# First stage of a three-stage decoder layer: squares and queries split in their PSUM banks, one LayerNorm sequence per tile, its output on ScalarE

## The chip, the cores and the metric

The kernel runs on one core of one Trainium2 chip, as a single launch. The metric is the device time of that launch in microseconds (us). The core has five engines that work side by side, each through its own instructions in a fixed order: TensorE (PE in the profile: matmuls, and PEld for the weight loads that run ahead of them), VectorE (DVE), ScalarE (ACT), GpSimd (POOL) and SyncE (SP), which here only issues DMAs. They hand work to each other by semaphores. SBUF is the working memory; PSUM, of 8 banks, takes the results of the matmuls.

## The reference, cut to what matters

The layer adds three blocks to a residual stream `x` of 4096 tokens by 512 channels. The change touches the first block alone:

```
h   = layernorm(x)                          # no gain, no bias
y   = (h - mean(h)) * rsqrt(var(h) + EPS)   # a second LayerNorm, on h
q   = (y * ln_g + ln_b) split in 4 heads of 128
s   = q @ k.T            # k: w_fc read as 2048 rows of 128
p   = square(relu(s))
x1  = x + (h + p @ v)    # v: w_proj.T read as 2048 rows of 128
```

The second block is attention to a context of 128 tokens, the third a shared and a routed feed-forward block with 32 experts. All is held to float32: a matmul of two float32 numbers is made as three matmuls of rounded parts, high by low, low by high and high by high.

## The kernel before, in words

**Tiles.** The first stage (`stage0`) takes the tokens in 8 tiles `t` of 512. For each tile and each of the 4 heads it runs 16 steps `kt`, one for each 128 rows of `k` and `v`: 512 steps in all. A step makes three matmuls into a PSUM bank `s` (L337), then ScalarE takes the relu into `rl` (L341), VectorE multiplies `s` by `rl` into `p`, which is the square (L343), and `split` parts `p` into a rounded high part `ph` and the rest `pl = p - ph`. Seven steps later (`LAG`) `av` feeds `ph` and `pl` to three matmuls (L298) that add up in the bank `o` of the head. A step is therefore six matmuls of 128 by 512.

**Who splits.** `split` (L93 to L96) makes the high part with a copy on ScalarE (L93), or on VectorE where it is told so (L95), and the low part with a subtraction on VectorE or GpSimd (L96). Of 8 steps in a row the numbers 1, 3, 5, 6 and 7 have the low part on GpSimd; 0, 2 and 4 have it on VectorE, and number 2 has its high part on VectorE too. [...]

**Buffers.** The banks of `s` go by turns: even `kt` have tag `P1`, odd `kt` have `P2`, two banks each; a bank is free for its next block of scores when nothing reads it any more. `p` lies in SBUF under tag `H` with 3 buffers, `rl` under `K` with 2, `ph` and `pl` under `A` and `B` with 8. Two more banks (`P4`) serve all transposes and the context products, two (`P3`) the sums `o`.

**LayerNorms of the next tile.** `prep` makes `y` for the next tile in the middle of the steps of the present one. It is a generator, and the loop over the steps takes one piece of it at a time. The tile has four row blocks of 128 tokens; two generators handle two blocks each, one after the other. A generator loads `x` (L236), takes mean and variance on VectorE (L241, L242), makes both LayerNorms' factors from them in a row of small operations (L246 to L251, the power on GpSimd, L248), writes `y` with VectorE (L254), then has GpSimd form the residual (L264), which SP stores to `x1` (L265). `prep_head` transposes `y` for one head (L272), applies gain and bias on ScalarE from PSUM to an SBUF tile `q` (L274), and splits `q` into `qh` and `ql`. Heads 0 to 2 of the next tile are made in step 12 of heads 1 to 3, the last one in step 8 of the tile itself.

**Background.** In some steps a further generator (`context_steps`) does a piece of preparation for the second stage: it splits weights with ScalarE and GpSimd, and makes products of the context (`ck`, `cv`) on TensorE.

**What sets the order.** A planner orders the instructions of each engine before the run: it goes by the order in which the program states them, by dependences, by free buffers and by its own estimates of durations. `g.after` keeps an instruction behind given ones on the same engine. On the chip each engine then follows its list, and an instruction that waits holds up everything behind it on its engine.

Of the kernel before, what the change touches and what calls it, by code (L numbers as in the profile page):

```python
# [8 lines left out]
F32 = mybir.dt.float32  # L9
# [5 lines left out]
A = mybir.AluOpType  # L15
AF = mybir.ActivationFunctionType
# [9 lines left out]
EPS = 1e-5  # L26
# [14 lines left out]
def f32(ap):  # L41
    return ap.bitcast(F32)
# [37 lines left out]
@contextmanager  # L80
def later(g, n):

    g.tc.cur_priority += n
    yield
    g.tc.cur_priority -= n


def split(g, hi, lo, src, lo_engine=None, hi_engine=None):

    if isinstance(lo_engine, cycle):  # L90
        lo_engine = next(lo_engine)
    if hi_engine is None:
        g.nc.scalar.copy(hi, src)  # L93
    else:
        hi_engine.tensor_copy(hi, src)  # L95
    (lo_engine or g.nc.vector).tensor_tensor(lo, src, f32(hi), A.subtract)  # L96
# [16 lines left out]
def weight_steps(g, dram, nk, width, name, lo_engine=None):  # L113
    hi, lo = ([[g.piece(name + z)[:] for _ in range(width // 512)] for _ in range(nk)] for z in "hl")
    yield from split_steps(g, dram, hi, lo, lo_engine)
    return hi, lo


def part(w, k, c):

    return w[k][c // 4][:, c % 4 * 128:c % 4 * 128 + 128]


def run(steps):

    try:
        while True:
            next(steps)
    except StopIteration as end:
        return end.value  # L130
# [31 lines left out]
def three(terms):  # L162

    (wh, wl), (xh, xl) = terms
    return (wl, xh), (wh, xl), (wh, xh)
# [53 lines left out]
def stage0(g, x, wfcT, wpT, lnT, x1, background):  # L219
    nc = g.nc  # L220
    NT = T // 512
    LAG = 7
    gb = g.c.tile([128, 2, 4], F32, name="gb")
    with later(g, 20):
        nc.sync.dma_start(gb[:], lnT)
    ys, qs = {}, {}

    def prep(t, tiles):

        rows = [slice(t * 512 + s * 128, t * 512 + s * 128 + 128) for s in tiles]
        n = len(rows)
        xt = [g.tile("G", "xt") for _ in rows]
        for v, r in zip(xt, rows):
            nc.sync.dma_start(v[:], x[r, :])  # L236
        yield
        mv = g.sm.tile([128, n, 2], F32, name="am", tag="am")
        for i, v in enumerate(xt):
            s6 = g.small("as", 6)  # L240
            nc.vector.bn_stats(s6[:], v[:])  # L241
            nc.vector.bn_aggr(mv[:, i, :], s6[:])  # L242
            yield
        ve, r0, tt, rs = (g.small("a" + z, 8) for z in "vptr")
        m = 2 * n
        nc.vector.tensor_scalar(ve[:, 0:n], mv[:, :, 1], EPS, None, A.add)  # L246
        nc.vector.tensor_scalar(ve[:, n:m], mv[:, :, 1], 1.0 + EPS, EPS * EPS, A.mult, A.add)
        power = nc.gpsimd.tensor_tensor(r0[:, 0:m], ve[:, 0:m], g.mhalf[:, 0:m], A.pow)  # L248
        nc.vector.scalar_tensor_tensor(tt[:, 0:m], r0[:, 0:m], -0.5, ve[:, 0:m], A.mult, A.mult)
        nc.vector.tensor_tensor(tt[:, 0:m], tt[:, 0:m], r0[:, 0:m], A.mult)  # L250
        nc.vector.scalar_tensor_tensor(rs[:, 0:m], tt[:, 0:m], 1.5, r0[:, 0:m], A.add, A.mult)  # L251
        for i, v in enumerate(xt):
            y = g.tile("C", "y")
            g.mark = nc.vector.tensor_scalar(y[:], v[:], mv[:, i, 0:1], rs[:, n + i:n + i + 1], A.subtract, A.mult)  # L254
            ys[t] = ys.get(t, []) + [y]
            if i % 2:
                yield

        sc, of = g.small("bv", 4), g.small("bp", 4)
        nc.vector.tensor_scalar(sc[:, 0:n], rs[:, 0:n], 1.0, None, A.add)  # L260
        nc.vector.scalar_tensor_tensor(of[:, 0:n], mv[:, :, 0], -1.0, rs[:, 0:n], A.mult, A.mult)
        for i, v in enumerate(xt):
            with g.after(power):
                g.kept = nc.gpsimd.tensor_scalar(v[:], v[:], sc[:, i:i + 1], of[:, i:i + 1], A.mult, A.add)  # L264
            nc.sync.dma_start(x1[rows[i], :], v[:])  # L265
            if i % 2:
                yield

    def prep_head(t, h):
        pt = g.bank("P4", "pt")  # L270
        for s in range(4):
            nc.tensor.transpose(pt[:, s * 128:(s + 1) * 128], ys[t][s][:, h * 128:(h + 1) * 128], g.ident)  # L272
        q = g.tile("J", "q")
        g.q = nc.scalar.activation(q[:], pt[:], AF.Identity, bias=gb[:, 1, h:h + 1], scale=gb[:, 0, h:h + 1])  # L274
        qh, ql = g.tile("E", "qh", FR), g.tile("F", "ql", FR)
        split(g, qh[:], ql[:], q[:])
        qs[t, h] = (qh, ql)

    run(prep(0, range(4)))
    steps = weight_steps(g, wfcT, 4, 512, "kw", cycle((nc.vector, nc.gpsimd)))  # L280
    kw = run(steps)
    prep_head(0, 0)
    prep_head(0, 1)
    with g.after(g.q):
        vw = run(weight_steps(g, wpT, 4, 512, "vw"))
    prep_head(0, 2)
    prep_head(0, 3)

    P, oT, cur = {}, {}, {}

    def av(t, h, kt):
        p = P.pop((t, h, kt))
        if kt == 0:
            cur["o"] = g.bank("P3", "o")
        o = cur["o"]
        j, rb = divmod(kt, 4)
        for n, (w, y) in enumerate(three(([part(v, rb, j) for v in vw], p))):
            nc.tensor.matmul(o[:], w, y[:], start=kt == 0 and n == 0, stop=kt == 15 and n == 2)  # L298
        if kt < 15:
            return  # L300
        oT[h] = g.tile("D", "oT")
        nc.scalar.copy(oT[h][:], o[:])
        if h < 3:
            return
        for s in range(4):
            rows = x1[t * 512 + s * 128:t * 512 + s * 128 + 128, :]
            b = g.tile("IJ"[s % 2] if t < NT - 1 else "G", "b")
            nc.sync.dma_start(b[:], rows)
            pt = g.bank("P4", "pt")
            for hh in range(4):  # L310
                nc.tensor.transpose(pt[:, hh * 128:(hh + 1) * 128], oT[hh][:, s * 128:(s + 1) * 128], g.ident)
            nc.vector.tensor_tensor(b[:], pt[:], b[:], A.add)
            nc.sync.dma_start(rows, b[:])

    steps = [(t, h, kt) for t in range(NT) for h in range(4) for kt in range(16)]
    todo = []
    marks = []
    for i, (t, h, kt) in enumerate(steps):
        if h == 0 and kt == 2 and t + 1 < NT:
            todo = [prep(t + 1, tiles) for tiles in ((0, 1), (2, 3))]  # L320
            for p in todo:
                next(p)
        if todo and (h > 0 or kt > 6):
            with g.after(*marks):
                if next(todo[0], True):
                    todo.pop(0)
        if t > 0 and h > 0 and kt % 8 == 6:
            with g.after(*marks):
                next(background, None)
        if h > 0 and t + 1 < NT and kt == 12:  # L330
            prep_head(t + 1, h - 1)
        if h == 0 and t > 0 and kt == 8:
            prep_head(t, 3)
        s = g.bank(("P1", "P2")[kt % 2], "s")
        j, rb = divmod(kt, 4)
        for n, (w, y) in enumerate(three(([part(k, j, rb) for k in kw], qs[t, h]))):
            nc.tensor.matmul(s[:], w, y[:], start=n == 0, stop=n == 2)  # L337
        if i >= LAG:
            av(*steps[i - LAG])
        r = g.tile("K", "rl")  # L340
        m0 = nc.scalar.activation(r[:], s[:], AF.Relu)  # L341
        p = g.tile("H", "p")
        m1 = nc.vector.tensor_tensor(p[:], s[:], r[:], A.mult)  # L343
        marks = [m0, m1]
        if (t, h, kt) == (NT - 1, 2, 0):
            g.marks = marks
        ph, pl = g.tile("A", "ph", FR), g.tile("B", "pl", FR)
        split(g, ph[:], pl[:], p[:], nc.gpsimd if i % 8 in (1, 3, 5, 6, 7) else None, nc.vector if i % 8 == 2 else None)
        P[t, h, kt] = (ph, pl)
    run(background)  # L350
    for st in steps[len(steps) - LAG:]:
        av(*st)
# [880 lines left out]
```

## Time and profile before

| what | us |
|---|---|
| median of three runs | 2747.65 (2745.44 to 2748.27) |
| the profiled execution | 2744.97, its span in the trace 2743.2 |
| first scores matmul / last of the stage's `o` matmuls start | 17.9 / 813 |
| PE busy over the span | 2681.9 |
| DVE, ACT, POOL busy over the span | 2054.2, 1786.0, 1033.7 |

The span runs from the first to the last instruction. In a group of the profile, the line number comes first, then the engine, the operation, the tile written and the tiles read, the shape, the count, the busy time in us and the mean duration in ns of one, and then the idle time of the engine just before such instructions and what ended it. A line L93, L95 or L96 is that of the helper `split`, so the tile names tell which split is meant. A matmul's recorded duration (0.39 us for one of 512 columns) is longer than the distance at which the next one starts (0.227 us), since they are pipelined: a busy PE includes that overlap.

### The profile page before, as it was taken

The numbers are of one execution on the slowest core, as the hardware profiler recorded it, in microseconds if no ns is written. First come the engines' busy times: TensorE is split into PE (matmuls) and PEld (weight loads), VectorE is DVE, ScalarE is ACT, GpSimd is POOL, SyncE is SP. The second block draws the span as 40 slices with busy tenths as digits, with TensorE's granted clock in tenths as the row PEclk, the third lists the DMA queues.
The fourth block names the chain that finished last, engine by engine and source line by source line (L and its number), as shares of the span: only waits on it lengthen the run. The fifth ranks groups of instructions, "written<-read, shape, count | busy, mean of one in ns | idle before, by whom it ended". The sixth has DMA issues, their size and how long they took to land. (4 is left out here: it accounts for less than half of the span.)

```text
span 2743.2 us, 47449 instructions
## 1 busy us (share of the span) xinstructions
PE 2681.9 (98%) x14788; PEld 2293.6 (84%) x14788; DVE 2054.2 (75%) x4671; ACT 1786.0 (65%) x3995; POOL 1033.7 (38%) x821
## 2 busy tenths in 40 slices
PE   7999999999999999999999999999999999999998
PEld 5877877777878999899997888888889888898886
DVE  8888788888887888888876722243777787778985
ACT  6777777787867777777775111133666676768885
POOL 5686566667653333333330030001223122223331
PEclk9999999999999999999999999999999999999999
DMA  4021112112120222322246222254888999899994
GB/s 141 32 70 70 70 62 72 64 58 81 36 70 33 75 90 90 114 78 91 74 138 207 96 93 101 72 173 109 271 265 277 284 302 298 280 279 287 325 316 140
DMA packets 237999, 396.69 MB, mean 145 GB/s; under 512 B 29376, under 2 KB 67280, under 8 KB 237744
## 3 DMA queue, kind: packets, MB, share of 16 engines
q1 hardware_dynamic: 223024, 366.45, 39.5%
q0 software_dynamic: 14720, 27.19, 5.0%
q8 instruction: 117, 1.92, 0.3%
q14 instruction: 138, 1.13, 0.1%
HBM read 311.67 MB, written 83.83 MB: 144 GB/s over the span
## 5 line engine op out<-in xcount | busy, mean ns | idle before, releaser
L96 DVE TENSOR_TENSOR rl<-raw,rh 128x512 fp32r<-128x512 f32 x768 | 510.5, 711 | 106.2 <-ACT rh L93 98.0
L93 ACT CAST rh<-raw 128x512 fp32r<-128x512 f32 x768 | 440.3, 622 | 135.7 <-DMA raw<-in_rg 82.8
L96 POOL TENSOR_TENSOR pl<-p,ph 128x512 fp32r<-128x512 f32 x320 | 427.4, 1344 | 242.9 <-ACT ph L93 219.0
L343 DVE TENSOR_TENSOR p<-s,rl 128x512 f32<-128x512 f32 x512 | 343.4, 683 | 81.5 <-ACT rl L341 62.0
L93 ACT CAST ph<-p 128x512 fp32r<-128x512 f32 x448 | 277.7, 622 | 153.9 <-DVE p L343 148.3
L341 ACT ACTIVATE rl<-s 128x512 f32<-128x512 f32 x512 | 301.3, 599 | 34.7 <-PE s L337 21.1
L1019 POOL DMA_INDIRECT out_dram<-v,idx x46 | 108.0, 2347 | 424.8 <-ACT v L1017 332.8
L448 ACT ACTIVATE e<-e,nm 128x128 f32<-128x128 f32 x512 | 199.2, 391 | 63.2 <-DVE nm L445 62.8
L451 POOL TENSOR_TENSOR e<-e,ri 128x512 f32<-128x512 f32 x128 | 133.5, 1043 | 245.2 <-DVE ri L449 128.3
L298 PE MATMUL o<-pl,vwh 128*128 128x512 f32 x512 | 208.0, 406 | 11.0 <-DVE pl L96 7.6
L337 PE MATMUL s<-qh,kwl 128*128 128x512 f32 x512 | 207.2, 406 | 7.3 <-DVE p L343 7.0
L337 PE MATMUL s<-qh,kwh 128*128 128x512 f32 x512 | 201.1, 393 | 0.0
L337 PE MATMUL s<-ql,kwh 128*128 128x512 f32 x512 | 201.1, 393 | 0.0
L298 PE MATMUL o<-ph,vwh 128*128 128x512 f32 x512 | 200.7, 392 | 0.0
L298 PE MATMUL o<-ph,vwl 128*128 128x512 f32 x512 | 198.8, 392 | 0.0
L96 DVE TENSOR_TENSOR pl<-p,ph 128x512 fp32r<-128x512 f32 x192 | 185.2, 965 | 16.1 <-ACT ph L93 13.7
L905 POOL DMA_INDIRECT x<-xs,idx x46 | 57.3, 1247 | 312.0 <-DMA raw<-in_rd 171.8
L93 ACT CAST hh<-s 128x512 fp32r<-128x512 f32 x92 | 57.0, 620 | 164.3 <-DVE s L760 117.2
L422 PE MATMUL q<-yh,wql 128*128 128x256 f32 x512 | 149.5, 292 | 2.8 <-DVE v L481 2.6
L422 PE MATMUL q<-yh,wqh 128*128 128x256 f32 x512 | 145.6, 284 | 0.0
L422 PE MATMUL q<-yl,wqh 128*128 128x256 f32 x512 | 145.0, 283 | 0.0
L755 PE MATMUL g<-z,sw 128*128 128x512 f32 x576 | 139.5, 390 | 1.7 <-ACT s L759 1.7
(296 smaller groups left out, 7607.9 us busy)
## 6 DMA issues: line engine op xcount, KB each, us to landing
raw<-in_rg SPq DMA_DIRECT2D x256, 256.0 KB, 5.3
raw<-in_ru SPq DMA_DIRECT2D x256, 256.0 KB, 5.1
raw<-in_rd SPq DMA_DIRECT2D x256, 256.0 KB, 4.7
z<-zT SPq DMA_DIRECT2D x128, 256.0 KB, 5.4
b<-x SPq DMA_DIRECT2D x64, 256.0 KB, 2.6
xt<-in_x SPq DMA_DIRECT2D x32, 256.0 KB, 2.7
x<-xt SPq DMA_DIRECT2D x32, 256.0 KB, 2.0
x<-b SPq DMA_DIRECT2D x32, 256.0 KB, 2.3
```

Of the source, the lines that this page charges most:

```text
L93: g.nc.scalar.copy(hi, src)
L96: (lo_engine or g.nc.vector).tensor_tensor(lo, src, f32(hi), A.subtract)
L298: nc.tensor.matmul(o[:], w, y[:], start=kt == 0 and n == 0, stop=kt == 15 and n == 2)
L337: nc.tensor.matmul(s[:], w, y[:], start=n == 0, stop=n == 2)
L341: m0 = nc.scalar.activation(r[:], s[:], AF.Relu)
L343: m1 = nc.vector.tensor_tensor(p[:], s[:], r[:], A.mult)
L422: nc.tensor.matmul(o[:, i, :], part(w, k, p), y[k // 2][:, k % 2, :], start=n == 0, stop=n == 11)
L448: nc.scalar.activation(e[:, hs], e[:, hs], AF.Exp, bias=nm[:, h:h + 1], scale=0.125, accum_out=su[:, h:h + 1])
L451: nc.gpsimd.tensor_tensor(e4, e4, ri[:].unsqueeze(2).to_broadcast([128, 4, 128]), A.mult)
L755: nc.tensor.matmul(p[:], part(w, k, c), y[k][:], start=n == 0, stop=n == 11)
L905: nc.gpsimd.indirect_dma_start(out=x[rows], out_offset=None, in_=xs, in_offset=bass.IndirectOffsetOnAxis(ap=idx[rows, b + j:b + j + 1], ax ...
L1019: nc.gpsimd.indirect_dma_start(out=out, out_offset=bass.IndirectOffsetOnAxis(ap=idx[rows, b + j:b + j + 1], axis=0), in_=v[rows], in_offse ...
```

## The change

In the steps where VectorE makes the low part (0, 2 and 4 of 8) the square is no longer written to an SBUF tile `p`: it goes back into its own PSUM bank `s`, and both parts are split from there. The other five steps keep `p`. In `prep_head` the query with gain and bias is likewise written back into the bank `pt` and split from there; the tile `q` is gone, so buffers `J` are left to `b`. `prep` treats all four row blocks of a tile as one sequence: one set of small operations on four blocks where there were two sets on two blocks, with the offset `-mean * factor` made for both LayerNorms at once (L251 after). `y` is made by ScalarE as `Identity(x * scale + bias)`; only in the first tile do blocks 1 and 3 stay on VectorE. The loop takes a piece of `prep` in every odd step where it took one in every step.

```diff
-    def prep(t, tiles):
-        rows = [slice(t * 512 + s * 128, t * 512 + s * 128 + 128) for s in tiles]
+    def prep(t):
+        rows = [slice(t * 512 + s * 128, t * 512 + s * 128 + 128) for s in range(4)]
...
-        ve, r0, tt, rs = (g.small("a" + z, 8) for z in "vptr")
-        nc.vector.tensor_scalar(ve[:, 0:n], mv[:, :, 1], EPS, None, A.add)
-        power = nc.gpsimd.tensor_tensor(r0[:, 0:m], ve[:, 0:m], g.mhalf[:, 0:m], A.pow)
...
+        ve, r0, tt, rs, of = (g.small("a" + z, 8) for z in "vptro")
+        nc.vector.tensor_scalar(ve[:, 0:4], mv[:, :, 1], EPS, None, A.add)
+        power = nc.gpsimd.tensor_tensor(r0[:], ve[:], g.mhalf[:], A.pow)
...
+        mean = mv[:, :, 0].unsqueeze(1).to_broadcast([128, 2, 4])
+        nc.vector.scalar_tensor_tensor(of[:].rearrange("p (a n) -> p a n", a=2), mean, -1.0,
+                                       rs[:].rearrange("p (a n) -> p a n", a=2), A.mult, A.mult)
+        if t > 0:
+            yield
         for i, v in enumerate(xt):
             y = g.tile("C", "y")
-            g.mark = nc.vector.tensor_scalar(y[:], v[:], mv[:, i, 0:1], rs[:, n + i:n + i + 1], A.subtract, A.mult)
+            if t == 0 and i % 2:
+                nc.vector.tensor_scalar(y[:], v[:], mv[:, i, 0:1], rs[:, 4 + i:5 + i], A.subtract, A.mult)
+            else:
+                nc.scalar.activation(y[:], v[:], AF.Identity, bias=of[:, 4 + i:5 + i], scale=rs[:, 4 + i:5 + i])
...
-        sc, of = g.small("bv", 4), g.small("bp", 4)
-        nc.vector.scalar_tensor_tensor(of[:, 0:n], mv[:, :, 0], -1.0, rs[:, 0:n], A.mult, A.mult)
+        sc = g.small("bv", 4)
...
-        q = g.tile("J", "q")
-        g.q = nc.scalar.activation(q[:], pt[:], AF.Identity, bias=gb[:, 1, h:h + 1], scale=gb[:, 0, h:h + 1])
+        g.q = nc.scalar.activation(pt[:], pt[:], AF.Identity, bias=gb[:, 1, h:h + 1], scale=gb[:, 0, h:h + 1])
-        split(g, qh[:], ql[:], q[:])
+        split(g, qh[:], ql[:], pt[:])
...
-            todo = [prep(t + 1, tiles) for tiles in ((0, 1), (2, 3))]
+            todo = prep(t + 1)
-        if todo and (h > 0 or kt > 6):
+        if t + 1 < NT and (h > 0 or kt > 6) and kt % 2:
...
-        p = g.tile("H", "p")
+        apart = i % 8 in (1, 3, 5, 6, 7)
+        p = g.tile("H", "p") if apart else s
         m1 = nc.vector.tensor_tensor(p[:], s[:], r[:], A.mult)
...
-        split(g, ph[:], pl[:], p[:], nc.gpsimd if i % 8 in (1, 3, 5, 6, 7) else None, nc.vector if i % 8 == 2 else None)
+        split(g, ph[:], pl[:], p[:], nc.gpsimd if apart else None, nc.vector if i % 8 == 2 else None)
```

More of the change, by code (lines that the diff above doesn't have):

```diff
@@ L226, in stage0 @@
     ys, qs = {}, {}
-    def prep(t, tiles):
-        rows = [slice(t * 512 + s * 128, t * 512 + s * 128 + 128) for s in tiles]
-        n = len(rows)
+    def prep(t):
+        rows = [slice(t * 512 + s * 128, t * 512 + s * 128 + 128) for s in range(4)]
         xt = [g.tile("G", "xt") for _ in rows]
@@ L237, in prep @@
         yield
-        mv = g.sm.tile([128, n, 2], F32, name="am", tag="am")
+        mv = g.sm.tile([128, 4, 2], F32, name="am", tag="am")
         for i, v in enumerate(xt):
@@ L243, in prep @@
             yield
-        ve, r0, tt, rs = (g.small("a" + z, 8) for z in "vptr")
-        m = 2 * n
-        nc.vector.tensor_scalar(ve[:, 0:n], mv[:, :, 1], EPS, None, A.add)
[L247 to L250, printed above, removed]
@@ L251, in prep @@
-        nc.vector.scalar_tensor_tensor(rs[:, 0:m], tt[:, 0:m], 1.5, r0[:, 0:m], A.add, A.mult)
+        ve, r0, tt, rs, of = (g.small("a" + z, 8) for z in "vptro")
+        nc.vector.tensor_scalar(ve[:, 0:4], mv[:, :, 1], EPS, None, A.add)
+        nc.vector.tensor_scalar(ve[:, 4:8], mv[:, :, 1], 1.0 + EPS, EPS * EPS, A.mult, A.add)
+        power = nc.gpsimd.tensor_tensor(r0[:], ve[:], g.mhalf[:], A.pow)
+        nc.vector.scalar_tensor_tensor(tt[:], r0[:], -0.5, ve[:], A.mult, A.mult)
+        nc.vector.tensor_tensor(tt[:], tt[:], r0[:], A.mult)
@@ L252, in prep @@
+        nc.vector.scalar_tensor_tensor(rs[:], tt[:], 1.5, r0[:], A.add, A.mult)
+        mean = mv[:, :, 0].unsqueeze(1).to_broadcast([128, 2, 4])
[3 more added lines that the diff above has]
+            yield
+        ys[t] = []
         for i, v in enumerate(xt):
             y = g.tile("C", "y")
-            g.mark = nc.vector.tensor_scalar(y[:], v[:], mv[:, i, 0:1], rs[:, n + i:n + i + 1], A.subtract, A.mult)
@@ L255, in prep @@
-            ys[t] = ys.get(t, []) + [y]
+            if t == 0 and i % 2:
+                nc.vector.tensor_scalar(y[:], v[:], mv[:, i, 0:1], rs[:, 4 + i:5 + i], A.subtract, A.mult)
+            else:
+                nc.scalar.activation(y[:], v[:], AF.Identity, bias=of[:, 4 + i:5 + i], scale=rs[:, 4 + i:5 + i])
+            ys[t].append(y)
             if i % 2:
                 yield
-        sc, of = g.small("bv", 4), g.small("bp", 4)
-        nc.vector.tensor_scalar(sc[:, 0:n], rs[:, 0:n], 1.0, None, A.add)
@@ L261, in prep @@
-        nc.vector.scalar_tensor_tensor(of[:, 0:n], mv[:, :, 0], -1.0, rs[:, 0:n], A.mult, A.mult)
+        sc = g.small("bv", 4)
+        nc.vector.tensor_scalar(sc[:], rs[:, 0:4], 1.0, None, A.add)
         for i, v in enumerate(xt):
             with g.after(power):
-                g.kept = nc.gpsimd.tensor_scalar(v[:], v[:], sc[:, i:i + 1], of[:, i:i + 1], A.mult, A.add)
+                nc.gpsimd.tensor_scalar(v[:], v[:], sc[:, i:i + 1], of[:, i:i + 1], A.mult, A.add)
             nc.sync.dma_start(x1[rows[i], :], v[:])
@@ L272, in prep_head @@
             nc.tensor.transpose(pt[:, s * 128:(s + 1) * 128], ys[t][s][:, h * 128:(h + 1) * 128], g.ident)
-        q = g.tile("J", "q")
-        g.q = nc.scalar.activation(q[:], pt[:], AF.Identity, bias=gb[:, 1, h:h + 1], scale=gb[:, 0, h:h + 1])
+        g.q = nc.scalar.activation(pt[:], pt[:], AF.Identity, bias=gb[:, 1, h:h + 1], scale=gb[:, 0, h:h + 1])
         qh, ql = g.tile("E", "qh", FR), g.tile("F", "ql", FR)
-        split(g, qh[:], ql[:], q[:])
+        split(g, qh[:], ql[:], pt[:])
         qs[t, h] = (qh, ql)
-    run(prep(0, range(4)))
+    run(prep(0))
     steps = weight_steps(g, wfcT, 4, 512, "kw", cycle((nc.vector, nc.gpsimd)))
@@ L315, in stage0 @@
     steps = [(t, h, kt) for t in range(NT) for h in range(4) for kt in range(16)]
-    todo = []
     marks = []
@@ L319, in stage0 @@
         if h == 0 and kt == 2 and t + 1 < NT:
-            todo = [prep(t + 1, tiles) for tiles in ((0, 1), (2, 3))]
-            for p in todo:
-                next(p)
-        if todo and (h > 0 or kt > 6):
+            todo = prep(t + 1)
+            next(todo)
+        if t + 1 < NT and (h > 0 or kt > 6) and kt % 2:
             with g.after(*marks):
-                if next(todo[0], True):
-                    todo.pop(0)
+                next(todo, None)
         if t > 0 and h > 0 and kt % 8 == 6:
```

## The prediction

> **What bounds the kernel now.** I read the page first: busy time of each engine over the span.
>
> ```profile
> span 2743.2 us, 47449 instructions
> ...
> PE 2681.9 (98%) x14788; PEld 2293.6 (84%) x14788; DVE 2054.2 (75%) x4671; ACT 1786.0 (65%) x3995; POOL 1033.7 (38%) x821
> ```
>
> TensorE is the bound, so an edit on the other engines is worth only the stalls it takes from TensorE or gives to it. Next, busy time by stretches, for the first stage between its start-up and its end (start:end, length, then busy time and count on PE, PEld, DVE, ACT, POOL):
>
> ```profile
> 26.00:812.00 786.00, 766.86 (x3435) 609.98 (x3434) 671.93 (x1102) 594.44 (x1145) 519.77 (x403) 1.00 0.18 61
> ```
>
> PE is idle for 786.0 - 766.9 = 19.1 us. That understates the loss, since a matmul is recorded for 0.39 us while the next starts after 0.227: each stall hides another 0.16. The waits of the same stretch name who is waited for (total us, times, longest):
>
> ```profile
> PEld s L337 <- DVE p L343: 20.4, 46, 1.9
> ...
> PEld o L298 <- DVE pl L96: 14.3, 19, 2.4
> ...
> PEld o L298 <- POOL pl L96: 10.9, 20, 1.0
> ...
> PEld pt L272 <- DVE y L254: 5.5, 13, 1.4
> ```
>
> Some 100 waits, so the loss is at most 19.1 + 100 x 0.16 = 35 us. From the start times in the timeline, counting each matmul that starts over 0.15 us late, I get 61 stalls and 29.7 us: 21.2 in seven clusters around the next tile's LayerNorms (near 42 to 59, 143 to 155, 233 to 251, 346 to 350, 440 to 452, 539 to 551, 640 to 654 us), 3.9 at 772 to 791, where the second stage's first LayerNorm runs, and 4.6 scattered. Nearly all end with VectorE. Why VectorE is late shows in its timeline in one cluster (start, us, then the idle time before it):
>
> ```profile
> 241.18 2.50 POOL L96 TENSOR_TENSOR pl<-p,ph 128x512 fp32r<-128x512 f32 x2
> 241.24 1.25 DVE L249 SCALAR_TENSOR_TENSOR at<-ap,av 128x4 f32<-128x4 f32 x1 [0.30 <-POOL ap L248]
> ...
> 242.51 1.18 DVE L250 TENSOR_TENSOR at<-at,ap 128x4 f32<-128x4 f32 x1
> ...
> 243.62 0.68 DVE L96 TENSOR_TENSOR pl<-p,ph 128x512 fp32r<-128x512 f32 x1
> ...
> 244.35 0.50 PE L298 MATMUL o<-pl,vwh 128*128 128x512 f32 x1 [2.02 <-DVE pl L96]
> ```
>
> Two operations on 4 columns take 1.25 and 1.18 us, just while GpSimd subtracts; TensorE then stands for 2 us. The large operations show the same (by tile, ns min/median/max; then the costliest DVE groups of the first 1300 us):
>
> ```profile
> L96 DVE TENSOR_TENSOR pl<-p,ph x192: 647/694/1791, 25.0 to 807.1; 128x512 fp32r<-128x512 f32 x192
> ```
>
> ```profile
> L343 DVE TENSOR_TENSOR p<-s,rl 128x512 f32<-128x512 f32 x512 | 343.4, 683 | 81.5 <-ACT rl L341 62.0 <-POOL pl L96 14.8 <-ACT vs L93 1.7
> ...
> L96 DVE TENSOR_TENSOR pl<-p,ph 128x512 fp32r<-128x512 f32 x192 | 185.2, 965 | 16.1 <-ACT ph L93 13.7 <-PE cv L205 0.7 <-PE s L337 0.3
> ...
> L96 DVE TENSOR_TENSOR pl<-pt,ph 128x512 fp32r<-128x512 f32 x96 | 65.1, 679 | 2.5 <-ACT ph L93 1.7 <-PE av L478 0.4
> ```
>
> The subtraction from SBUF has a mean of 965 ns over a median of 694; the one whose source lies in PSUM (`pt`, second stage) means 679, and the product `p<-s,rl`, which reads PSUM too, never exceeds 694 in 512 instances.
>
> [...] 1791 ns at most with two SBUF inputs, 694 with one in PSUM. [...] That concerns the copy of step 2, 427 ns in the median from SBUF; no float32 copy of this size from PSUM is in the trace. [...] So a bank holding `p` is closed to its next scores until the subtraction ends.
>
> **The change part by part**, counted for the stretch above (seven tiles' LayerNorms).
>
> VectorE. Low parts from PSUM: 191 x (966 - 679) = -54.8 us. `y` leaves: 28 x 713 = -20.0. `ql` from PSUM: 28 x (892 - 679) = -6.0. Small operations L246 to L251, L260, L261: 14 sets of 291 + 157 + 870 + 757 + 302 + 316 + 149 = 2842 ns become 7: -19.9. The copy of step 2 from PSUM: 64 x (683 - 577) = +6.8, at the price of the product; at the least 0. The product written to PSUM shows nowhere: I take its 683; 100 ns more, 192 times, would add 19, and a gain of as much has nothing for it. Sum -94: 672 falls to 578 us, 85% to 74% of the stretch.
>
> ScalarE. `y` arrives: 28 at the 782 ns of `q<-pt,gb`, the form with two pointer operands [...]: +21.9. Casts from PSUM at the 582 of `ph<-pt` where SBUF took 622 and 627: -(128 x 40 + 28 x 45) = -6.4. Writing `q` to PSUM: taken at its present 782. Sum +15.5: 594 to 610 us, 76% to 78%.
>
> GpSimd: 14 powers at 1.22 become 7 at the first tile's 1.67, -5; its subtractions (mean 1344, median 1297) may lose their tail. The four residuals of a tile now stand in one row, 4 x 0.86 = 3.4 us, behind which its low parts wait; it waits 219 us for `ph` in this stage, which covers this but for some tenths. SP: the same loads and stores; stores of `x1` come some ten steps later, and `x1` is not read until the tile's own end, 64 steps on. Behind them on SP stand background loads with six buffers. I cost both at nothing; if that cover fails, background pieces come later, within a stage that has spare steps for them.
>
> None of this is time by itself. What counts is TensorE's margin. In the planned order a bank of scores is reused a median of 21 matmuls = 4.78 us after its last one, before and after. Before, it is free after 0.16 + relu 0.60 + product 0.68 and handovers 0.1 = 1.5: margin 3.2. After, for steps 0, 2 and 4: 0.16 + 0.60 + 0.68, one other product ahead of the subtraction 0.68, cast 0.58 (beside that product, mostly), subtraction 0.68, handovers 0.2: 3.0 to 3.6, margin 1.2 to 1.8. The undisturbed steady state still runs without a stall.
>
> Disturbances. In the planned order all four `y` of a tile stand next to each other on ScalarE: 4 x (0.78 - 0.09 overlap) = 2.8 us, with `oT` (0.59) behind them, or one step further on, and in four tiles a background cast (0.61 to 0.63) nearby. Behind them wait the casts of two steps, and the matmuls on `ph` and banks behind those. Of 3.4 to 4.0 us, the margin takes 1.2 to 1.8; transposes (0.4 to 0.9 us) and in three tiles context products (1.3 to 2.7 us) keep TensorE busy meanwhile. Left: 0 to 2 us, I take 1.1, x 7 = 8. On VectorE one set of small operations is left where there were two, and 74% load in place of 85%: 0.45 a tile, 3 in all. So 21.2 becomes 11. The scattered 4.6 lose the late subtractions but meet the smaller margin: 3. The 3.9 at the end stay. Start-up: `y` on two engines takes 1.6 us in place of 1.9, less 0.15 for the offset: 0.2 gained. Holding `pt` through its split (+1.3 us, 32 times, of two banks): 0, at most 9 if each tile stalls once.
>
> Sum: -10.2 - 1.6 - 0.2 = -12 us. The profiled execution took 2744.97 (span 2743.2 and 1.8 around it), so 2733; the median of the runs is 2.7 above it: 2735.7. Instructions from the second stage's start on stand in the same order, so the gain is carried through.
>
> **Rivals.** (1) ScalarE gives back what VectorE frees: bursts of 2 us a tile, `pt` holds and scattered stalls add up to 26 again: 2742 to 2753. For it: 78% load in a fixed order; against: the background products. (2) Slower: the smaller margin decides. If ScalarE's queue delays the casts of in-place steps by over 1.8 us, every such bank is late. There are some 20 extra ScalarE operations per tile (`q`, `qh`, `oT`, casts); if a third of the 192 in-place steps lose 0.5 us, that is 32, less some 17 gained on VectorE's side: 2763. Against: extras come singly, 0.6 us. (3) VectorE was all of it: of 29.7 only the 3.9 remain: 2722. That the edits do not take hold is excluded by the planned order, which shows them.
>
> **Numbers.** Likeliest, a gain of 4 to 22 us: 0.60. Rival 1: 0.17. Rival 2: 0.17. Rival 3: 0.06. Between executions a change under 0.2%, 5.5 us, can't be told from none. Faster: 0.62; same: 0.20; slower: 0.18. The likeliest's own range is 2726 to 2744; 8 in 10, taking in rivals, is 2718 to 2757.
>
> **What would show it.** Right: `pl<-s,ph` near 680 ns without a tail; DVE under 600 us in the stretch; 28 `y` on ACT near 0.78; waits of PE for DVE down by half, waits for ACT new after each `y` row. Wrong: `s<-s,rl` well over 683; PE waiting for in-place banks (scores after `pl<-s,ph`) in tiles' quiet steps; losses over 2 us at each `y` row.

## The result, and the profile after

The changed kernel takes 2718.83 us (median of 4 runs, 2715.42 to 2721.65); the kernel before, beside it, 2746.55 (4 runs, 2744.37 to 2748.27). The ratio is 0.9899, with a 95% interval of 0.9887 to 0.9912: 27.7 us faster. The forecast was 2735.7 with a range of 2718 to 2757, so the sign was right, the time came out inside the range by less than 1 us, and the gain was more than twice the 12 us of the sum.

The page of the changed kernel, busy time of each engine over the span:

```profile
span 2718.4 us, 47027 instructions
...
PE 2668.8 (98%) x14788; PEld 2297.3 (85%) x14788; DVE 1968.7 (72%) x4592; ACT 1803.6 (66%) x4025; POOL 1004.2 (37%) x814
```

The same number of matmuls has 13 us less of busy time (of those with 512 columns, 0.39 us in the median, 154 were over 0.45 us in the first stage before and 109 are now), and VectorE has lost 85 us. Where the time went is read from the stretches, here the first stage from 26 us to its end, and all that follows (start:end, length, busy time and count on PE, PEld, DVE, ACT, POOL, then clock and DMA):

```profile
26.00:787.00 761.00, 752.57 (x3434) 613.54 (x3434) 590.10 (x1025) 612.16 (x1175) 488.29 (x395) 1.00 0.19 62
787.00:2718.00 1931.00, 1907.00 (x11324) 1676.78 (x11323) 1364.78 (x3539) 1178.05 (x2830) 507.58 (x406) 1.00 0.56 177
```

The stage took 786 us and now takes 761. Before, what followed lasted from 812 to 2743 us, 1931 us as well: the gain lies in the first stage and is carried through. By the last `o` matmul, at 813.2 us before and 789.1 after, 24.1 of the 24.8 us between the two spans are gained there. TensorE's idle time in the stretch fell from 19.1 to 8.4 us. Counted as the prediction counts, by how late each matmul starts, the stalls over 0.15 us fell from 29.7 to 12.6 us, and those between 0.06 and 0.15 us, which the prediction left out, from 17.1 to 11.3. The waits of TensorE's weight loads between 26 and 795 us (total us, times, longest):

```profile
PEld s L339 <- DVE p L347: 10.0, 18, 1.5
PEld s L339 <- DVE pl L96: 4.3, 7, 1.5
PEld o L303 <- ACT ph L93: 2.7, 4, 0.8
PEld o L303 <- POOL pl L96: 2.4, 7, 1.0
PEld pt L278 <- DVE ql L96: 1.7, 1, 1.7
PEld pt L278 <- ACT y L261: 0.9, 2, 0.5
```

The wait for VectorE's products has halved (20.4 to 10.0). The waits for its low parts (14.3 before an `o` matmul) are gone, and so is most of that for GpSimd's (10.9 to 2.4). What the change brings in is there as well and small: banks that are closed until their low part is made (4.3), late casts (2.7), a `pt` bank held by its query (1.7, once), late `y` (0.9). The costliest groups of the first stage after start-up:

```profile
L347 DVE TENSOR_TENSOR s<-s,rl 128x512 f32<-128x512 f32 x191 | 132.7, 695 | 89.9 <-ACT rl L343 89.4
L96 DVE TENSOR_TENSOR pl<-s,ph 128x512 fp32r<-128x512 f32 x192 | 131.2, 683 | 21.4 <-ACT ph L93 18.8
...
L261 ACT ACTIVATE y<-xt,ao,ar 128x512 f32<-128x512 f32 x28 | 20.5, 807 | 1.6 <-DVE ao L251 1.6
...
L96 DVE TENSOR_TENSOR ql<-pt,qh 128x512 fp32r<-128x512 f32 x29 | 19.7, 678 | 0.8 <-ACT qh L93 0.8
```

The subtraction from the bank has a mean of 683 ns where the one from SBUF had 965, and none of the 192 takes over 695. What is left of the old trouble shows in the timeline of one tile (start, us, idle time before):

```profile
630.14 1.29 POOL L96 TENSOR_TENSOR pl<-p,ph 128x512 fp32r<-128x512 f32 x1 [3.00 <-ACT ph L93]
630.20 1.26 DVE L267 TENSOR_SCALAR bv<-ar 128x4 f32<-128x4 f32 x1
...
631.37 0.68 DVE L347 TENSOR_TENSOR p<-s,rl 128x512 f32<-128x512 f32 x1
...
632.10 0.19 PEld L339 LDWEIGHTS s<-qh,kwl 128*128 128x128 f32 x1 [0.87 <-DVE p L347]
```

An operation on 4 columns still takes 1.26 us beside a subtraction on GpSimd; the product behind it is late, and TensorE waits for the bank.

### The profile page after: what moved, and what is told of

The parts are those of the page before. It is cut to its first block, busy times and chain, and to the rows that moved or that the text cites. A ratio compares the mean times of both kernels' runs of the same rounds, so it can differ in the third digit from the quotient of the medians.

```text
span 2718.4 us, 47027 instructions
## 1 busy us (share of the span) xinstructions
PE 2668.8 (98%) x14788; PEld 2297.3 (85%) x14788; DVE 1968.7 (72%) x4592; ACT 1803.6 (66%) x4025; POOL 1004.2 (37%) x814
## 5 line engine op out<-in xcount | busy, mean ns | idle before, releaser
L96 POOL TENSOR_TENSOR pl<-p,ph 128x512 fp32r<-128x512 f32 x320 | 411.3, 1296 | 270.1 <-ACT ph L93 212.9
L343 ACT ACTIVATE rl<-s 128x512 f32<-128x512 f32 x512 | 292.9, 603 | 39.8 <-PE s L339 33.6
L347 DVE TENSOR_TENSOR p<-s,rl 128x512 f32<-128x512 f32 x320 | 215.2, 683 | 41.7 <-ACT rl L343 39.3
L93 ACT CAST ph<-p 128x512 fp32r<-128x512 f32 x320 | 199.1, 626 | 63.8 <-DVE p L347 61.2
L303 PE MATMUL o<-pl,vwh 128*128 128x512 f32 x512 | 202.5, 395 | 0.5 <-POOL pl L96 0.5
L347 DVE TENSOR_TENSOR s<-s,rl 128x512 f32<-128x512 f32 x192 | 133.4, 695 | 89.9 <-ACT rl L343 89.4
L96 DVE TENSOR_TENSOR pl<-s,ph 128x512 fp32r<-128x512 f32 x192 | 131.2, 683 | 21.4 <-ACT ph L93 18.8
```

## The experiments

The change has three parts: squares of steps 0, 2 and 4 in their banks (called **squares**), queries in their bank (**queries**), and one LayerNorm sequence per tile with `y` on ScalarE (**norms**). Theory: the gain is VectorE's waiting for GpSimd, which all three parts reduce, and ScalarE's row of four `y` costs part of it. Rivals: the gain comes from the buffers of `p` (the product waited 14.8 us for GpSimd to free one); the row of `y` or the thinner margin of the banks eats it. Each kernel below ran five rounds beside the kernel before, whose median was 2744.97 for the first four changed kernels of the table, 2746.31 for the next four, 2746.55 for the changed kernel itself and 2746.56 for the last ones; where two medians are subtracted below, up to 1.6 us of the difference can be that. Stalls are counted in the first stage of one trace each. In some traces matmuls start at half rate for a while (every 0.43 us in place of 0.227; see the last section) and count as stalls: 1.2 to 1.6 us before, in squares, in queries, in norms and in "all, `y` on VectorE", 2.4 with the residuals in four pieces, 3.5 in norms with `y` on VectorE, 3.8 in squares and norms, none in the others:

| kernel | us | ratio to before (95%) | gain, us | stalls over 0.15 us | of 0.06 to 0.15 |
|---|---|---|---|---|---|
| before | | 1 | 0 | 29.7 | 17.1 |
| squares | 2736.87 | 0.9971 (0.9961 to 0.9981) | 8.1 | 27.0 | 12.1 |
| queries | 2752.46 | 1.0028 (1.0017 to 1.0039) | -7.5 | 34.0 | 18.5 |
| norms, `y` on VectorE | 2739.14 | 0.9977 (0.9968 to 0.9986) | 5.8 | 32.6 | 12.4 |
| norms | 2736.56 | 0.9969 (0.9957 to 0.9981) | 8.4 | 26.0 | 14.7 |
| squares, queries | 2735.48 | 0.9962 (0.9948 to 0.9975) | 10.8 | 25.6 | 12.3 |
| queries, norms | 2739.49 | 0.9976 (0.9967 to 0.9984) | 6.8 | 29.1 | 13.8 |
| squares, norms | 2727.89 | 0.9925 (0.9911 to 0.9939) | 18.4 | 22.3 | 10.3 |
| all, `y` on VectorE | 2728.58 | 0.9932 (0.9919 to 0.9946) | 17.7 | 21.4 | 9.6 |
| all (the changed kernel) | 2718.83 | 0.9899 (0.9887 to 0.9912) | 27.7 | 12.6 | 11.3 |
| all, squares in SBUF buffers of their own | 2734.40 | 0.9964 (0.9952 to 0.9976) | 12.2 | 23.0 | 13.2 |
| squares, norms, residuals in four pieces | 2726.68 | 0.9929 (0.9916 to 0.9941) | 19.9 | 18.3 | 10.9 |
| all, `y` in four pieces | 2723.02 | 0.9917 (0.9904 to 0.9929) | 23.5 | 14.2 | 11.8 |
| all, small operations on GpSimd | 2716.48 | 0.9891 (0.9877 to 0.9905) | 30.1 | 8.5 | 9.3 |

**One part alone: squares.**

```diff
-        p = g.tile("H", "p")
+        apart = i % 8 in (1, 3, 5, 6, 7)
+        p = g.tile("H", "p") if apart else s
```

> Only the squares of steps 0, 2 and 4 go back into their bank; queries and LayerNorms as before. If VectorE's collisions with GpSimd in the subtraction are the main cause, this alone gives 14 to 20 us of the 28, with the low parts of these steps near 683 ns in place of 965. If the LayerNorm sequences are the main cause, it gives 3 to 8. If the smaller margin of the banks costs what it was feared to, it is no faster than before.

Measured 2736.87, a gain of 8.1 us, well under the 14 to 20 that the theory expected. The low part's mean is 684 ns, without a tail, so the whole relief of 54 us on these subtractions is here; it is worth 8. Some of it moves elsewhere: the small operations, still two sets a tile, now take 50.7 us where before they took 39.8. And there are new waits of weight loads:

```profile
PEld s L337 <- DVE pl L96: 10.5, 12, 1.6
PEld o L298 <- ACT ph L93: 8.3, 11, 2.0
```

The first is the thinner margin of the banks, which rival 2 feared: it is real while `y` and two sets of small operations are still on VectorE, but costs less than the relief brings. The second, casts that come late for an `o` matmul, is also new (0.2 us before); its cause was not isolated.

**One part alone: queries.**

```diff
-        q = g.tile("J", "q")
-        g.q = nc.scalar.activation(q[:], pt[:], AF.Identity, ...)
+        g.q = nc.scalar.activation(pt[:], pt[:], AF.Identity, ...)
-        split(g, qh[:], ql[:], q[:])
+        split(g, qh[:], ql[:], pt[:])
```

> Only the queries go back into their bank. 28 subtractions lose 0.2 us each on VectorE, 6 us in all, little of it on TensorE's path: a gain of 0 to 3 us. If the longer hold of the transposes' banks costs anything, it shows here alone: slower by up to 9 us.

Measured 2752.46: 7.5 us slower, the only part that loses by itself. `ql` behaves as meant (from the bank, its longest is under 0.7 us; before, 1.59), and the longer hold of the bank, which the expectation named for a loss, shows as one wait of 0.3 us. The loss lies elsewhere: from 735 us on, where the second stage's first LayerNorm meets the last steps, stalls are 9.0 us against 3.9 before. The two other kernels that have the queries in banks and the squares of steps 0, 2 and 4 in SBUF show the same there (8.2 and 8.6); all the rest have 3.4 to 4.1. These three traces also share one order of that LayerNorm's operations on VectorE, which no other has, and in it three or four of the first six passes over `xt` take about 1.5 us beside GpSimd, where before two do. So some 5 of the 7.5 us go with an order that the planner chose; why this edit makes it choose so is open.

**One part alone: norms, with `y` on VectorE and on ScalarE.** Both are the changed kernel with squares and queries as before; the first has in addition

```diff
-            if t == 0 and i % 2:
+            if True:
                 nc.vector.tensor_scalar(y[:], v[:], ...)
```

> Only the LayerNorms of a tile are one sequence; its output stays on VectorE, squares and queries as before. If the number of small operations in the row is what makes the clusters of stalls, this gives 5 to 9 us. If it is the output on VectorE (20 us of its time), it gives 0 to 3.

> The LayerNorms as in the changed kernel, output on ScalarE; squares and queries as before. By the LayerNorm theory 12 to 16 us faster than before. If the squares carry most of it, 5 to 10. If the row of four outputs on ScalarE costs about 8 us, it is no better than the same with the output on VectorE.

Measured 2739.14 and 2736.56. One sequence alone is worth 5.8 us, as expected if the number of small operations matters, and moving `y` another 2.6, which the intervals don't tell from nothing here. The two together stay under the 12 to 16 us of the LayerNorm theory. Unlooked for is the longest `ql` subtraction: 1.59 us before, 1.83 with `y` on ScalarE, 6.67 with `y` on VectorE.

**One part undone: the squares, the queries.** The changed kernel with one edit taken back each, in the lines shown above.

> The changed kernel with the squares alone undone: all low parts of VectorE have two SBUF inputs again. If parts add up (+7.5 and -8.4 us alone), about as before, -4 to +3 us. If the loss of the queries alone came from their meeting with the old LayerNorm sequences, 8 to 14 us faster than before. Low parts of VectorE are back near 960 ns.

> The changed kernel with the queries alone undone, so squares in place and one LayerNorm sequence with its output on ScalarE. By themselves these two gave 8.1 and 8.4 us. If parts simply add up, this is 16 to 17 us faster than before. If squares in place thin the banks' margin so much that VectorE's LayerNorm work eats their gain unless it is cut as well, the two together give more than their sum: 22 to 30. If instead the queries are what binds the parts, it stays under 17.

Neither result lies in a range that was expected for it. Without the squares 2739.49, so beside the other two they are worth 20.7 us (2739.49 - 2718.83), against 8.1 alone; 4.7 of the 20.7 are the stalls after 735 us (8.2 against 3.5). Without the queries 2727.89: there they are worth 9.1, where alone they cost 7.5. Squares and norms without queries give 18.4, about their sum (8.1 + 8.4 = 16.5). Most of the rest lies around one wait that the queries' edit prevents. The timeline of the kernel without it:

```profile
640.66 4.29 DVE L96 TENSOR_TENSOR ql<-q,qh 128x512 fp32r<-128x512 f32 x1
640.67 3.74 POOL L96 TENSOR_TENSOR pl<-p,ph 128x512 fp32r<-128x512 f32 x3
...
644.88 0.68 DVE L348 TENSOR_TENSOR p<-s,rl 128x512 f32<-128x512 f32 x1
...
645.61 0.50 PE L340 MATMUL s<-qh,kwl 128*128 128x512 f32 x1 [2.65 <-DVE p L348]
```

GpSimd is late here (since 635.17 it has done four residuals and two background subtractions without a pause), so three low parts follow one another, and the subtraction of a query with two SBUF inputs stands through all three: 4.29 us in place of 0.68. The products behind it are late, and TensorE waits 2.65 us. Stalls between 615 and 672 us are 7.9 us in this kernel and 2.9 in the changed one: 5.0 of the 9.1 us. The changed kernel has the same row on GpSimd,

```profile
637.04 3.81 POOL L96 TENSOR_TENSOR pl<-p,ph 128x512 fp32r<-128x512 f32 x3
```

but no `ql` subtraction over 0.7 us. Another 2.6 us are thirteen matmuls at half rate from 26.7 to 31.8 us, right after start-up, which the changed kernel doesn't have; that they have to do with the queries is not shown.

**One part undone: the norms; `y` back on VectorE.**

> Squares and queries in place, LayerNorms as before. If parts add up (-8.1 and +7.5 us alone), as before within 3 us. If the queries' loss came from VectorE's collisions, which the squares remove, 8 to 14 us faster. Stalls of TensorE at the LayerNorm clusters stay, near 20 us.

> The changed kernel with the LayerNorm output of all tiles back on VectorE. If the row of four outputs on ScalarE costs about 8 us, as the prediction put it, this is faster than the changed kernel by up to 5 us. If VectorE's share of the clusters is what counts with the thin margin, it gives back 6 to 12 of the 28 us.

Without the norms 2735.48: they are worth 16.7 us beside the other two, against 8.4 alone. Added to the squares, the queries don't lose (10.8 us against 8.1), and the stalls after 735 us are 3.5 here. With the sequence kept but `y` on VectorE 2728.58, so the row of `y` on ScalarE, which the prediction put down as a cost, gains 9.8. The group and the wait of that kernel say why:

```profile
L259 DVE TENSOR_SCALAR y<-xt,am,ar 128x512 f32<-128x512 f32 x28 | 25.0, 950 | 0.0
```

```profile
PEld pt L278 <- DVE y L259: 9.5, 14, 1.2
```

On VectorE a `y` takes 950 ns here, and transposes wait 9.5 us for it; on ScalarE that wait is 0.9. That it is long because it meets GpSimd is taken from the kernel before: there the 18 `y` that ran beside no GpSimd instruction took 536 ns in the mean (507 to 547), and nine that ran beside one for over 0.1 us took 1085.

**The rival on buffers.** The changed kernel with the squares of steps 0, 2 and 4 in SBUF, in two buffers that GpSimd never reads:

```diff
-        p = g.tile("H", "p") if apart else s
+        p = g.tile("H" if apart else "J", "p")
-            b = g.tile("IJ"[s % 2] if t < NT - 1 else "G", "b")
+            b = g.tile("I" if t < NT - 1 else "G", "b")
```

> The changed kernel, but the squares of steps 0, 2 and 4 go to SBUF again, into two buffers of their own that GpSimd never reads, so that the product no longer waits for GpSimd to free a buffer; the subtraction has two SBUF inputs again. Nothing is left out. If the gain of the squares in their banks is the collision of that subtraction with GpSimd (my theory): its mean is 900 to 990 ns with a tail above 1700, and the time is 2732 to 2742 us, as with the squares in the shared buffers (2739.5). If it is the buffers (the product waited 14.8 us for GpSimd before): that wait is under 2 us here too and the time is 2717 to 2724 us.

Measured 2734.40. Its groups in the first stage:

```profile
L347 DVE TENSOR_TENSOR p<-s,rl 128x512 f32<-128x512 f32 x502 | 338.1, 684 | 84.1 <-ACT rl L343 75.2 <-POOL pl L96 6.1
L96 DVE TENSOR_TENSOR pl<-p,ph 128x512 fp32r<-128x512 f32 x189 | 177.2, 939 | 23.2 <-ACT ph L93 21.5 <-PE o L303 0.2 <-PE pt L316 0.2
```

The product's wait for buffers has more than halved (14.8 to 6.1), and at best 5.1 of the squares' 20.7 us come with it (2739.49 - 2734.40; the two intervals overlap). The collision is back in full: 939 ns. So up to 15.6 us (2734.40 - 2718.83) go with the bank and not with the buffers of `p`. Two orders of the planner stay mixed in. The stalls after 735 us, 8.6 here, make 5.1 of the 15.6. And with squares in banks the planner also takes most of the stage's blocks of scores in another order, the odd `kt` of a pair before the even one, and without it doesn't: the relu of an even step starts only after the odd step's scores in 206 of 256 pairs of the changed kernel's trace, and in 106 of this one's. No run holds these orders and moves the squares, so what they are worth is open. (`b` also has two buffers here in place of four.)

**The residuals' row.** Squares and norms, queries as before, and the four residuals of a tile taken in four pieces of work:

```diff
             nc.sync.dma_start(x1[rows[i], :], v[:])
-            if i % 2:
+            if i % 2 or t > 0:
                 yield
```

> The kernel with the squares and the LayerNorms changed and the queries as before (2727.9 us), but with the four residuals of a tile on GpSimd in four pieces of work instead of two. If the queries cost time there because GpSimd, behind on its work after a row of residuals, runs without a pause while the subtraction of a query waits for it (my theory): the longest ql subtraction falls from 4.3 us to 2.6 or less, the stalls near 615 to 672 us fall from 7.9 to 3 to 5 us, and the time is 2721 to 2725 us. If the row of residuals does not matter: longest subtraction over 3.5 us, time 2726 to 2730 us.

Measured 2726.68 (ratio 0.9929, 0.9916 to 0.9941), against 2727.89 without the edit. GpSimd's timeline:

```profile
631.60 3.04 POOL L270 TENSOR_SCALAR xt<-xt,bv,ao 128x512 f32<-128x512 f32 x4
```

The four still stand in one row here, as in every tile: the planner put them together again. The longest `ql` is 4.31 us as before. The run therefore doesn't test the row, though its time is the one that was expected if the row does not matter; that GpSimd's lateness comes from it is argued from the timeline only.

**The row of `y` spread.**

```diff
             ys[t].append(y)
-            if i % 2:
+            if i % 2 or t > 0:
                 yield
```

> The changed kernel, but with each y of a tile in a piece of work of its own, so that ScalarE no longer runs four in a row. If the row delays the casts behind it (the term of 8 us in the prediction): a gain of 3 to 8 us over the changed kernel, 2711 to 2716 us. If the row costs nothing, because the margin and the context products cover it: 2717 to 2721 us, and PE's stalls over 0.15 us stay at 11 to 14 us.

Measured 2723.02, which neither reading had (its interval and the changed kernel's overlap a little). The rows of four are broken (three and one, or two, one and one), and nothing is gained: stalls are 14.2 in place of 12.6 us, waits for casts 4.2 in place of 2.7. The row of four costs nothing that spreading recovers; the last `y` comes 2 to 7 us later, and with it the transposes and, by 5 to 9 us, the residuals. That the loss of 4.2 us comes from this is not shown.

**The small operations on GpSimd.** In the changed kernel, all that lies between the statistics and `y`, and the residual's scale, on GpSimd, with the three combined operations written as simple ones:

```diff
-        nc.vector.tensor_scalar(ve[:, 0:4], mv[:, :, 1], EPS, None, A.add)
+        nc.gpsimd.tensor_scalar(ve[:, 0:4], mv[:, :, 1], EPS, None, A.add)
...
-        nc.vector.scalar_tensor_tensor(tt[:], r0[:], -0.5, ve[:], A.mult, A.mult)
-        nc.vector.tensor_tensor(tt[:], tt[:], r0[:], A.mult)
-        nc.vector.scalar_tensor_tensor(rs[:], tt[:], 1.5, r0[:], A.add, A.mult)
+        nc.gpsimd.tensor_tensor(tt[:], r0[:], ve[:], A.mult)
+        nc.gpsimd.tensor_tensor(tt[:], tt[:], r0[:], A.mult)
+        nc.gpsimd.tensor_scalar(tt[:], tt[:], -0.5, 1.5, A.mult, A.add)
+        nc.gpsimd.tensor_tensor(rs[:], tt[:], r0[:], A.mult)
```

> The changed kernel, but with the nine small operations of a tile's LayerNorm between the statistics and y on GpSimd, beside the power, in place of VectorE. Nothing is left out. If what remains of the stalls around the LayerNorms (8.5 us) comes from VectorE's small operations waiting for GpSimd: those stalls fall to 2 to 4 us and the time to 2711 to 2715 us. If GpSimd's longer row then delays its own low parts: PE waits for POOL pl rise from 2.4 to 5 us or more and the time is 2718 to 2726 us.

Measured 2716.48, between the two expected ranges and the fastest here, though its interval overlaps the changed kernel's. Its waits between 26 and 795 us:

```profile
PEld s L341 <- DVE p L349: 5.7, 7, 1.3
PEld s L341 <- DVE pl L96: 4.5, 7, 1.5
PEld o L305 <- POOL pl L96: 1.8, 5, 0.6
```

The wait for products falls from 10.0 to 5.7, GpSimd's low parts are not later (1.8), and the stalls around the LayerNorms go from 8.5 to 4.7 us, where 2 to 4 were expected. On GpSimd each of these operations takes 0.20 to 0.24 us. The stage ends 5.9 us earlier (last `o` matmul 783.2 against 789.1), of which the span keeps 4.0: what follows takes 1.9 us more. At start-up the small operations now stand between GpSimd's weight subtractions, and the first `y` comes at 15.3 in place of 13.4 us. So by these two traces about half of what was left around the LayerNorms was VectorE's small operations.

## Why the prediction was right in sign and short in size

That the time lies in the stated range is in part luck: it is outside of the 2726 to 2744 of the likeliest reading, and the wider range took in rivals that did not come true as they were told.

Against its own time, the profiled execution went from 2744.97 to 2720.27, 24.7 us; the forecast for it was 2733, 12.7 too high. The other 4.1 of the miss is the step from that execution to the median: 2.7 was added, and the profiled run of the changed kernel was 1.4 above its median.

**The bound and the place: right.** TensorE is the bound (busy 98% of the span), the gain is its stalls, nearly all ended by VectorE, and the rest of the kernel takes the same 1931 us.

**VectorE's sum: right but for the small operations.** The low parts gave 185.2 - 131.2 = 54.0 us (forecast 54.8), `ql` took 678 ns (679), the copy 687 (683, an estimate at the product's time), so +7.0 (+6.8). The product into PSUM takes 695, 12 ns more, 2.3 us in all. The step that failed here is "14 sets become 7: -19.9". They gave 13.2 (39.8 to 26.6 us): the time of such an operation is mostly its wait for GpSimd (before, up to 1.29 us beside a GpSimd instruction, 0.12 to 0.17 without one), and one set meets it as well (`av` went from 291 to 903 ns in the mean). So VectorE came to 590 us, not 578.

**ScalarE's sum: near.** `y` takes 807 ns, not 782; casts from PSUM 593, not 582; writing the query to PSUM 758, below its 782. Together 594 to 612 us, where 610 was forecast.

**The row of four `y`: the mis-sized term.** "1.1, x 7 = 8" and 3 for small operations made 21.2 into 11; measured, 8.5. Of it the small operations make about 4, by the last experiment (3 was forecast), which leaves at most 4.7 for the rows and all else, in place of 8. Casts (2.7) and `y` (0.9) that TensorE waits for are 3.6 together. The prediction's own cover, context products and transposes between the matmuls, may have been taken too low; no run isolates it. It also compared the row with nothing, where the other place for `y` costs 9.8 us more.

**Scattered stalls: 3 forecast, 0.7 measured.** The smaller margin didn't cost what the late subtractions left: in the undisturbed steps no matmul waits for a bank's low part, and the seven such waits (4.3 us) stand at start-up, around the LayerNorms and in the last steps. The last 3.9 us stayed, at 3.5. **Start-up: 0.2 forecast as a gain**; the first scores matmul comes 0.4 later (17.9 to 18.3).

**Left out: stalls under 0.15 us.** They fell by 5.8. With 2.5 at the LayerNorms, 2.3 scattered and 0.4 at the end this gives 11.0 of the 12.7. The remaining 1.7, and 0.6 by which the start-up came out worse than forecast, are in the spacing of matmuls too fine to count as stalls. For the same reason "at most 19.1 + 100 x 0.16 = 35 us" was no bound: by start times the two classes before are 29.7 + 17.1 = 46.8 us.

**The bank of queries: "0, at most 9" right, but not its worth.** The hold cost one wait of 1.7 us. The prediction saw in this part 6 us of VectorE's time; by the runs it costs 7.5 alone and is worth 9.1 beside the other two. Nothing in the sum could show that, since parts were added as if each met the same neighbours in the same planned order. "GpSimd: the four residuals ... I cost both at nothing" holds only with the queries in banks: without, GpSimd's backlog is where the longest wait stands.

**The rivals.** The nearest was the third, only the last 3.9 us of stalls left, at 2722, with a chance of 0.06. Its stalls did not come down that far (12.6), but the fine ones did too. Rival 1 had the sign of ScalarE's part wrong. Rival 2's wait for banks is there in the squares alone (10.5 us) and fades to 4.3 once `y` and half of the small operations are gone from VectorE.

## What to carry to other kernels

Where VectorE and GpSimd got in each other's way, a mean far above the median told it (965 over 694 ns for the low parts), and the price was not the sum of the lengthened durations (54 us on these subtractions, worth 8.1 alone) but what stood behind the longest of them. Parts that relieve the same contention can't be priced one by one: the value of each here ranged from a loss of 7.5 to a gain of 9 us, or from 8 to 21, with what stood beside it. Some 5 us of that loss, and 5 of the 21, come with another planned order in the last steps, so compare the order of operations before reading a difference as the worth of an edit. An operand in PSUM took VectorE's large subtractions out of the contention (683 ns in place of 965), and ScalarE was the better place for a pass that VectorE does faster when undisturbed (807 ns on ScalarE; on VectorE 536 undisturbed, 950 as it ran).

## What the runs showed of the hardware that was not expected

**A wait through several instructions.** With both inputs in SBUF, VectorE's subtraction took up to 1.79 us beside a GpSimd subtraction of 1.30, where 0.69 is the median. At times it took much longer: the one of the kernel without the queries stood through a row of three on GpSimd that followed without a pause (4.29 us), and the longest in the norms with `y` on VectorE took 6.67 us. It was not so each time. In the kernel before, a subtraction that met a row was let in after the first instruction of it, and the next ones on GpSimd took longer instead (3.45 us for two that take 1.30 each elsewhere):

```profile
162.29 1.30 POOL L96 TENSOR_TENSOR pl<-p,ph 128x512 fp32r<-128x512 f32 x1 [0.83 <-ACT ph L93]
162.37 1.77 DVE L96 TENSOR_TENSOR pl<-p,ph 128x512 fp32r<-128x512 f32 x1
...
163.55 3.45 POOL L96 TENSOR_TENSOR wkl<-raw,wkh 128x512 fp32r<-128x512 f32 x2
```

What decides between the two is open.

**Small operations.** With 4 columns, 1.26 us beside a GpSimd subtraction of 1.29 in the changed kernel, against 0.15 for like operations that are undisturbed; the same kind on GpSimd took 0.20 to 0.24.

**The clock after a stall.** In the kernel without the queries, after the wait that ends at 645.61 us, the stretches give the granted clock (the third figure from the end):

```profile
642.00:646.00 4.00, 1.35 (x5) 0.83 (x6) 4.00 (x3) 1.47 (x4) 2.41 (x2) 1.00 0.71 243
646.00:650.00 4.00, 4.00 (x13) 3.07 (x12) 2.67 (x6) 1.49 (x4) 1.28 (x1) 0.57 0.00 0
```

For about 3 us, matmuls start every 0.43 us in place of 0.227, so after this stall of 2.65 us another 1.4 are lost (seven matmuls by 0.2). The length of one wait doesn't settle it: in the kernel before, one of 2.02 us that ends at 244.35 is followed by a granted clock of 1.00 up to 252 us, while the same kernel has one of 0.57 from 650 to 654 us after waits of at most 0.95 us in the 4 us ahead. What does settle it is not shown. Comparing the stalls of two traces, look for such stretches first: the kernel before lost 1.2 us in this one, the changed kernel has none in the first stage.
